# Layer 0 of a graph and experts kernel: the last two second runs of experts go from 160 rows to 128

## The chip, the cores and the metric

The kernel runs on one core of one Trainium2 chip. The metric is the device time of one execution, in microseconds (us). Five engines work side by side, each with its own queue of instructions: TensorE (PE, whose weight loads are listed apart as PEld), VectorE (DVE), ScalarE (ACT), GpSimd (POOL) and SyncE (SP, which here only issues transfers). They meet through semaphores. Transfers between the chip's memory and its on-chip buffers run on 16 DMA engines, fed by queues of SP, ACT and POOL.

## The reference

Two layers, each a graph step and a mixture of experts, on `x` of 3327 tokens with 256 features. All arithmetic is float32. Layer 0, in which the change lies:

```python
x = x + gnn(layernorm(x), adj)                 # a@h / deg @ W.T + b
h = layernorm(x)
probs = softmax(h @ gate_w + gate_b)           # 16 experts
top_probs, top_idx = top_k(probs, 2)           # each token goes to 2 experts
hidden = silu(h @ w1[e]) * (h @ w2[e])         # 256 -> 512
x = x + sum over its 2 experts of prob * (hidden @ w3[e])   # 512 -> 256
```

The reference computes all experts for all tokens and selects; the kernel computes only the two that a token chose. So 2 x 3327 = 6654 pairs of token and expert are spread over 16 experts, 416 each in the mean, and how many each gets depends on the inputs. They come from fixed random seeds.

Layer 1 has a graph attention step and six experts of another form; the change does not touch it.

## The kernel before

**Tiles.** The 3327 tokens make 26 tiles of 128 (the last has 127). Tiles are handled in chunks of four. The graph step runs in three blocks of chunks; the first two (`GRAPH0[:2]`) are tiles 0 to 15, that is tokens 0 to 2047.

**Routing.** When a chunk's graph output is done, `dispatch` chooses two experts per token and writes each pair into a list in memory (`list0`), which has a region of 3328 places for every expert. After tile 15, `filled` (L399) lifts the counter of every expert that has fewer than 256 pairs to 256, so that pairs of later tokens are placed from place 256 on. Places without a pair hold a neutral entry: weight 0, token 0, and as its target one of 256 spare rows behind the result.

**Slots.** The experts' work is done in slots (`plan`, L969). A slot gathers up to 256 rows by its list (`rows_in0`, POOL, L1040), turns them (L1053), multiplies by w1 and w2 (`hidden0`, L1065), applies silu and the product (L1069, L1073), multiplies by w3 (`out0`, L1088), scales (L1093) and adds the rows to the result `xd` in memory (POOL scatter with addition, L1095). There are 32 usual slots:

- slots 0 to 9: the first 256 places of experts 0 to 9, begun while the graph step's last block is being finished;
- slots 10 to 21: experts 10 to 15, which are ranked by their counts (`rank_table`, L409); for each rank one slot of 256 rows and one for its rest;
- slots 22 to 31: the rests of experts 0 to 9, ranked likewise.

The rest of an expert is what stands from place 256 on. How many rows a rest slot takes is fixed by its rank in `WIDTHS`, L100 and L101: six numbers for slots 11, 13, ... 21, then ten for slots 22 to 31. Each slot is cut into parts of 128 rows (`parts0`, L1032): a width of 160 is one part of 128 and one of 32, each with its own gather, turning, w3 matmuls, scaling and scatter.

**The spill table.** `spill_table` (L431) subtracts the width of its rank (`cap`) from each expert's rest. For whatever is left it counts tiles of 256, rounded up, and lists them. Column 3 of its output tells whether there is any. All five engines load that number (`asked`, L562, at slot 30) and branch on it after slot 31 (`more`, L572; the call is at L1236, the branch instructions are recorded at L575). If it is 0, the body is skipped. If it is 1, the body runs: two spill slots of 256 rows, slots 32 and 33, whatever number of pairs they hold, with all parts of a slot; then a second question, whether there are more than two tiles (column 5), and a further body for those; and then, for the six tiles of `HEAD`, a load from `xd`, a layer norm and the weighting that prepares them for layer 1 (`loaded1`, L1158; `weighted1`, L1164).

In the usual case those six tiles are prepared earlier, beside slots 28 to 31 (`head1`, L1189), with loads made on the condition that nothing spills; the graph step of layer 1 can then begin as soon as slot 31 is done. The remaining tiles (`REST`) are loaded after slot 31's scatter has landed.

**What orders the work.** Each engine takes its instructions in the order in which the program was recorded. On POOL, gathers and scatters share one queue, and each waits there for what it needs. A usual slot's scatter waits for its own scaled rows and for the other half of the slot before (`x_added`, `waits`, L1101 to L1105). Spill slots write to `xd` as a whole, so each of their scatters waits for the landing of the one before. On SP, an instruction that waits holds up all loads behind it.

Of the kernel before, what the change touches and what calls it, by code (L numbers as in the profile page):

```python
# [19 lines left out]
P = 128  # L20
# [5 lines left out]
def kernel(  # L26
# [70 lines left out]
    SA = 2 * P  # L97
    AHEAD_E = 5 * E0 // 8
    SHARED = E0 - AHEAD_E
    WIDTHS = [SA, SA - 32, SA - 64, SA - 64, SA - 96, SA - 96]  # L100
    WIDTHS += [SA, SA - 32, SA - 32, SA - 64, SA - 64, SA - 64, SA - 64, SA - 96, SA - 96, SA - 96]  # L101
    assert len(WIDTHS) == E0 and NP % SA == 0
    USUAL0 = 2 * E0
    LATE0 = USUAL0 - 5
    FEW0 = USUAL0 + 2
    SLOTS0 = USUAL0 + (2 * N + E0 * (SA - 1 - min(WIDTHS))) // SA

# [323 lines left out]
    def spill_table(rank, rest, head):  # L431
# [4 lines left out]
        def small(name, w=E0, dtype=F32):  # L436
            return work.tile([P, w], dtype, name=name, bufs=1)

        cap, t, d, end, hot, at = small("x_cap"), small("x_t"), small("x_d"), small("x_end"), small("x_hot"), small("x_at", 2)
        nc.vector.memset(cap, float(WIDTHS[0]))  # L440
        for i in range(1, E0):
            if WIDTHS[i] != WIDTHS[i - 1]:
                nc.vector.tensor_scalar(t, rank, float(i), float(WIDTHS[i] - WIDTHS[i - 1]), op0=OP.is_ge, op1=OP.mult)
                nc.vector.tensor_tensor(cap, cap, t, op=OP.add)
# [1030 lines left out]
```

## Time and profile before

| what | value |
|---|---|
| time, median of 3 runs | 1006.41 us (1002.47 to 1008.44) |
| time of the profiled execution | 1003.44 us |
| its span, first to last instruction | 1001.4 us |
| mean granted TensorE clock | 0.973 |
| busy: PE, PEld, DVE, ACT, POOL | 927.9, 780.5, 486.5, 280.8, 435.4 us |
| layer 0's slots on PE | about 197 to 573 us |
| PE busy in 328 to 573 us | 239.1 of 245 us |
| first matmul of layer 1's graph step | 573.43 us |

How to read it: times are counted from the start of the span. A row of a group names line, engine, operation, tile written and tile read, shapes and how often, then busy time and mean duration, then the idle time of the engine ahead of them and what ended it. In a timeline the first number is the start, the second the duration of merged rows, and what stands in brackets is idle time ahead of it and its releaser. One matmul of the program on float32 data shows as two records of PE. A transfer issued by POOL has a short record on POOL (its issue); when its data have landed is seen from who waits for it.

### The profile page before, as it was taken

The page shows a single profiled execution, that of the slowest core. Times are in us where ns is not written, and L with a number is a line of the kernel's source. Part 1 is how long each engine was busy: PE and PEld are TensorE (multiplying, and loading weights), DVE is VectorE, ACT ScalarE, POOL GpSimd, SP SyncE. Part 2 cuts the span into 40 slices and gives each one's busy share as a digit, 9 for nine tenths or more (in the row PEclk, how much of TensorE's full clock was granted, in tenths as well). Part 3 has the DMA queues.
Part 4 walks back from the last instruction along what each step waited for, and adds up shares of the span by engine and source line. Part 5 has one row for each costly group of instructions (what it writes and reads, how often), then busy time and mean ns, then how long its engine had stood idle before and what let it go on. Part 6 is the DMA issues. An engine that isn't in the chain of part 4 may idle for free. (4 is left out here: it accounts for less than half of the span.)

```text
span 1001.4 us, 14307 instructions
## 1 busy us (share of the span) xinstructions
PE 927.9 (93%) x4506; PEld 780.5 (78%) x4506; DVE 486.5 (49%) x1788; ACT 280.8 (28%) x634; POOL 435.4 (43%) x407
## 2 busy tenths in 40 slices
PE   6899999999998899999999899999999899799981
PEld 5677878778897689888888677787778688678870
DVE  6575585244623222221212657576674764435663
ACT  3311331034311111111111524244132644234330
POOL 2040062522477444545454321000452777777761
PEclk9999999998999899999999999999999999999996
DMA  9998677856676466666988479888975222442376
GB/s 333 327 304 305 232 203 225 257 171 194 170 177 169 124 183 181 178 169 163 263 261 235 132 231 304 287 288 320 269 190 169 61 64 61 66 95 91 96 256 210
DMA packets 104945, 200.56 MB, mean 200 GB/s; under 512 B 30436, under 2 KB 59558, under 8 KB 104864
## 3 DMA queue, kind: packets, MB, share of 16 engines
q1 hardware_dynamic: 64002, 150.87, 46.1%
q0 software_dynamic: 20528, 30.56, 14.2%
q10 hardware_dynamic: 20334, 18.17, 5.7%
q8 instruction: 36, 0.59, 0.2%
q14 instruction: 45, 0.37, 0.1%
HBM read 170.39 MB, written 35.47 MB: 206 GB/s over the span
## 5 line engine op out<-in xcount | busy, mean ns | idle before, releaser
L831 PE MATMUL acc<-big,y 128*128 128x512 f32 (+2 forms) x1456 | 340.2, 388 | 20.7 <-DVE big L705 13.1
L831 PEld LDWEIGHTS acc<-big,y 128*128 128x128 f32 (+1 forms) x1456 | 262.7, 192 | 78.5 <-issue 14.0
L1065 PE MATMUL acc<-xT,w 128*128 128x256 f32 (+3 forms) x1024 | 215.9, 364 | 0.0
L1065 PEld LDWEIGHTS acc<-xT,w 128*128 128x128 f32 x1024 | 187.2, 201 | 17.3 <-issue 3.5
L384 POOL DMA_INDIRECT list<-where,t_idx x104 | 110.6, 1063 | 148.7 <-DVE t_idx L381 96.5
L705 DVE TENSOR_SCALAR big<-adj 128x1536 fp32r<-128x1536 int32 (+5 forms) x128 | 111.3, 873 | 100.1 <-DMA adj<-in_adj_t 55.1
L1088 PE MATMUL acc<-w,hid 128*128 128x256 f32 (+3 forms) x512 | 118.3, 381 | 0.0
L1073 DVE TENSOR_TENSOR hid<-hid,acc 128x512 f32<-128x512 f32 (+3 forms) x64 | 40.0, 624 | 149.4 <-PE acc L1065 142.3
L1095 POOL DMA_INDIRECT xd<-y,who x44 | 68.8, 1563 | 100.1 <-DVE y L1093 58.5
L1088 PEld LDWEIGHTS acc<-w,hid 128*128 128x128 f32 (+3 forms) x512 | 89.2, 178 | 20.5 <-issue 3.9
L1069 ACT ACTIVATE hid<-acc 128x512 f32<-128x512 f32 (+3 forms) x64 | 35.0, 547 | 207.1 <-PE acc L1065 193.8
L627 POOL DMA_INDIRECT zd<-y,who x58 | 71.5, 1233 | 27.8 <-DVE y L1323 12.2
L1309 ACT ACTIVATE h<-acc,v 128x256 f32<-128x256 f32 x116 | 54.8, 473 | 90.9 <-PE acc L1306 90.4
L601 POOL DMA_INDIRECT xg<-hd,who x58 | 59.5, 1027 | 42.3 <-issue 36.2
L1306 PE MATMUL acc<-h,v 128*128 128x256 f32 x232 | 60.6, 384 | 1.8 <-ACT h L1309 1.8
L1306 PE MATMUL acc<-xT,v 128*128 128x256 f32 x232 | 60.7, 383 | 0.0
L1095 POOL DMA_INDIRECT xd<-y,whos x20 | 32.3, 1616 | 65.0 <-DVE y L1093 46.9
L289 POOL TENSOR_TENSOR ln_var<-ln_var,half 128x2 f32<-128x2 f32 (+2 forms) x19 | 16.0, 844 | 100.7 <-DVE ln_var L287 77.6
L1318 PE MATMUL acc<-v,h 128*128 128x256 f32 x232 | 59.7, 403 | 0.1
L1321 DVE TENSOR_TENSOR y<-acc,v 128x512 f32<-128x512 f32 x29 | 20.0, 690 | 69.4 <-PE acc L1318 69.4
L1306 PEld LDWEIGHTS acc<-h,v 128*128 128x128 f32 x232 | 44.3, 199 | 9.1 <-ACT h L1309 2.6
L1040 POOL DMA_INDIRECT xg<-hd,who x44 | 43.0, 976 | 17.8 <-issue 11.0
(300 smaller groups left out, 987.9 us busy)
## 6 DMA issues: line engine op xcount, KB each, us to landing
adj<-in_adj_t SPq DMA_DIRECT2D x58, 768.0 KB, 5.9
w<-in_ffn_w SPq DMA_DIRECT2D x78, 512.0 KB, 6.5
adj<-in_adj_t SPq DMA_DIRECT2D x25, 639.5 KB, 5.8
adj<-in_adj_t SPq DMA_DIRECT2D x25, 512.0 KB, 4.9
adj<-in_adj_t SPq DMA_DIRECT2D x12, 767.0 KB, 5.7
hd<-ln_h ACTq DMA_DIRECT2D x12, 512.0 KB
w_all<-w1d SPq DMA_DIRECT2D x6, 898.0 KB, 7.8
w1d<-in_ffn_w ACTq DMA_DIRECT2D x18, 256.0 KB, 4.9
```

The costliest lines, as they stand in the source:

```text
L384: ins = nc.gpsimd.indirect_dma_start(out=rows_of[2 * (t0 + j) + i], out_offset=bass.IndirectOffsetOnAxis(ap=idx[:, i, j : j + 1], axis=0), ...
L601: last["pool"] = nc.gpsimd.indirect_dma_start(out=xg[:, h, :], out_offset=None, in_=of, in_offset=bass.IndirectOffsetOnAxis(ap=who[:, h, 1 ...
L627: last["pool"] = nc.gpsimd.indirect_dma_start(out=zviews[n * s + h], out_offset=bass.IndirectOffsetOnAxis(ap=who[:, h, 0:1], axis=0), in_= ...
L705: last["mask"] = nc.vector.tensor_scalar(mask[:kr, :, :cols], a[:kr, :, :cols], value, None, op0=op)
L831: last["graph"] = nc.tensor.matmul(acc[c][k][:, :w], y[:kr, j, part, k * P : (k + 1) * P], mask[:kr, jj, i0 : i0 + w], start=(j == 0 and p ...
L1040: last["pool"] = nc.gpsimd.indirect_dma_start(out=xg[:m, h, :], out_offset=None, in_=hd_of[0][: NE0 * P, :] if s < AHEAD_E else hd[:, :], ...
L1065: last["slot"] = nc.tensor.matmul(q[:, c, :n], w[:, k, h0 : h0 + 2 * P - 1 : 2], xT[:, k, :n], start=(k == 0), stop=(k == KD - 1))
L1088: nc.tensor.matmul(ps[:m, h, :], hid[c // 2][:, c % 2, h * P : h * P + m], w3[:, c // 2, c % 2, :], start=(c == 0), stop=(c == NC0 - 1))
L1095: ins = last["pool"] = nc.gpsimd.indirect_dma_start(out=xd_of[2 + h] if s < USUAL0 else xd, out_offset=bass.IndirectOffsetOnAxis(ap=who[s] ...
L1306: ins = nc.tensor.matmul(ps[:, c, :], w[:, k, c : H1 : NC1], src[:, k, :], start=(k == 0), stop=(k == 1))
L1309: last["act"] = nc.scalar.activation(dst[:, c, :], ps[:, c, :], AF.Relu, bias=early["w"][s % 3][:, BB + 2 * i + c : BB + 2 * i + c + 1])
L1318: nc.tensor.matmul(ps[:, h, :], h2[:, c, h * P : (h + 1) * P], w[:, c, :], start=(c == 0), stop=(c == NC1 - 1))
```

## The change

Two numbers in `WIDTHS` change: the rest of the emptiest of experts 10 to 15 (slot 21) and that of the emptiest of experts 0 to 9 (slot 31) are given 128 rows instead of 160.

```diff
-    WIDTHS = [SA, SA - 32, SA - 64, SA - 64, SA - 96, SA - 96]
-    WIDTHS += [SA, SA - 32, SA - 32, SA - 64, SA - 64, SA - 64, SA - 64, SA - 96, SA - 96, SA - 96]
+    WIDTHS = [SA, SA - 32, SA - 64, SA - 64, SA - 96, P]
+    WIDTHS += [SA, SA - 32, SA - 32, SA - 64, SA - 64, SA - 64, SA - 64, SA - 96, SA - 96, P]
```

Three things follow in the program:

- slots 21 and 31 have one part instead of two, and their w1 and w2 matmuls are 128 columns wide instead of 160;
- `spill_table` has two more steps in its sequence of widths (four more small DVE instructions), and treats as spilled what the two rests have above 128;
- `SLOTS0`, which uses the smallest width, goes from 63 to 65, which lengthens the innermost body by two slots.

These are the functions that use the numbers:

```python
def parts0(s):
    n = plan[s][-1]
    return [(h, min(P, n - h * P)) for h in range(-(-n // P))]

# in spill_table; rest = count - 256
nc.vector.tensor_tensor(t, rest, cap, op=OP.subtract)
nc.vector.tensor_scalar(nt, t, float(SA - 1), 0.0, op0=OP.add, op1=OP.max)
nc.vector.tensor_scalar(nt, nt, SA.bit_length() - 1, None, op0=OP.arith_shift_right)
...
nc.vector.tensor_scalar(out[:, 3:4], end[:, E0 - 1 :], 0.0, m, op0=OP.is_gt, op1=OP.max)
nc.vector.tensor_scalar(out[:, 5:6], end[:, E0 - 1 :], float(FEW0 - USUAL0), None, op0=OP.is_gt)

# after the usual slots
with more(*early["more"]):
    list(slots0(USUAL0, FEW0))
    with more(*asked(early["spill"], 0, 5, "many")):
        list(slots0(FEW0, SLOTS0))
    for g in HEAD:
        loaded1(g)
        weighted1(pools1[0], g, norm(g))
```

## The prediction

> **What bounds the kernel now.** First the page's groups by line.
>
> ```profile
> span 1001.4 us, 14307 instructions
> PE 927.9 (93%) x4506; PEld 780.5 (78%) x4506; DVE 486.5 (49%) x1788; ACT 280.8 (28%) x634; POOL 435.4 (43%) x407
> ...
> L1095 POOL DMA_INDIRECT xd<-y,who x44 | 68.8, 1563 | 100.1 <-DVE y L1093 58.5
> ...
> L1095 POOL DMA_INDIRECT xd<-y,whos x20 | 32.3, 1616 | 65.0 <-DVE y L1093 46.9
> ...
> L1040 POOL DMA_INDIRECT xg<-hd,who x44 | 43.0, 976 | 17.8 <-issue 11.0
> ```
>
> PE sets the pace. The scatters number 44 + 20 = 64, two for each of 32 slots: nothing spills today, the body behind the branch is skipped. Next, PE's timeline at slots 19 to 22, which tells what a narrow slot costs.
>
> ```profile
> 463.61 2.35 PE L1065 MATMUL acc<-xT,w 128*128 128x160 f32 x16
> 465.79 3.62 PE L1088 MATMUL acc<-w,hid 128*128 128x256 f32 x16
> 469.24 2.34 PE L1065 MATMUL acc<-xT,w 128*128 128x160 f32 x16
> 471.42 0.60 PE L1053 MATMUL mm<-ident,xg 128*128 128x128 f32 x4
> 471.86 3.65 PE L1065 MATMUL acc<-xT,w 128*128 128x256 f32 x16
> 475.34 3.73 PE L1088 MATMUL acc<-w,hid 128*128 128x256 f32 x16
> ```
>
> Rows follow without gaps: slot 21 is bound by PE. A half of its hidden layer takes 2.17 us from start to start (463.61 to 465.79), its w3 product (475.34) 3.7 us. Third, the passage from layer 0 to layer 1.
>
> ```profile
> 572.95 0.48 DVE L1093 TENSOR_SCALAR y<-acc,who 128x256 f32<-128x256 f32 x1 [0.22 <-PE acc L1088]
> 573.43 0.50 PE L831 MATMUL acc<-big,y 128*128 128x512 f32 x1 [0.52 <-ACTq L575]
> 574.94 1.56 POOL L1095 DMA_INDIRECT xd<-y,who  x1 [3.75 <-DVE y L1093]
> 576.14 34.10 PE L831 MATMUL acc<-big,y 128*128 128x512 f32 x141 [2.20 <-DVEq L575]
> 576.80 1.34 POOL L1095 DMA_INDIRECT xd<-y,who  x1 [0.30 <-issue]
> 581.46 1.42 SPq L1162 DMA_DIRECT2D xs<-xd  x3
> 586.79 0.74 DVE L284 BATCH_NORM_STATS2 ln_st<-xs 128x6 f32<-128x256 f32 x2
> ```
>
> Slot 31 ends on PE at 572.9, layer 1's graph step begins 0.5 us later and runs on, because its first six tiles were prepared before; the last scatter lands beside it. Fourth, that stretch in windows: after the busy times come the granted clock (third number from the end), the DMA engines' share and their GB/s.
>
> ```profile
> 576.00:578.00 2.00, 1.86 (x4) 1.49 (x5) 0.00 (x0) 0.00 (x0) 1.70 (x2) 0.50 0.52 67
> 578.00:580.00 2.00, 2.00 (x7) 1.58 (x6) 0.00 (x0) 0.00 (x0) 0.14 (x1) 0.66 0.26 28
> ```
>
> After 3 us of near idleness PE got half its clock until about 579.3. Fifth, the branch, L575; the two times behind the durations are the starts of its first and second passing, and the first is ours.
>
> ```profile
> L575 SPq COMPARE_BRANCH x2: 73/73/73, 559.3 to 976.7; - x2
> L575 POOLq COMPARE_BRANCH x2: 63/70/77, 575.3 to 982.0; - x2
> L575 POOLq INC_SWDGE_SEM x2: 1153/1177/1201, 580.1 to 985.5; - x2
> ```
>
> SP reaches the branch at 559, long before POOL.
>
> **Does anything spill?** No view tells counts, so I worked them out from the reference's inputs, in double precision, with the lifting to 256 after token 2047. The rests of experts 10 to 15, ranked, are 203, 175, 160, 160, 134, 132; those of experts 0 to 9 are 255, 200, 184, 177, 172, 165, 160, 155, 149, 140. All fit today's widths, which agrees with the 64 scatters. Of the new ones two don't: 132 is 4 above 128, 140 is 12. That is one tile each, two together: column 3 becomes 1, column 5 (more than two) stays 0. The body runs with two full slots for 16 pairs. For both to fit, 16 pairs would have to choose otherwise; the smallest distance between a token's second and third choice is 4.5e-5 in the logits, so one or two may.
>
> **What the Trainium skill says.** "TensorE: Matmul & The Clock Gate", in "Part 1: The HAM clock gate", has PE fall to 1.2 GHz after an idle window of about 3.4 us and return after as much work; the 0.50 above agrees. The same page's "LDWEIGHTS (loading the stationary operand)" gives columns / 1.2 ns, 107 ns for 128, which bounds narrow matmuls from below. "DMA: Bandwidth & Descriptors", "Anatomy of one DMA — SWDGE (gpsimd) path", gives about 2.0 us fixed for a transfer from POOL, most of it until the write is confirmed; the trace has more: scatters land 3.7 us after their start at the least, 6.5 in the median.
>
> **The change part by part**, on the clock of the profiled execution.
>
> 1. Narrow slots. A half goes from 2.17 to about 1.74 us (256, 192 and 160 columns took 3.57, 2.71 and 2.17; 16 weight loads of 107 ns are 1.71), twice 0.43; eight of 16 w3 records go, 1.8; two turnings 0.2. So 2.9 us a slot, 5.8 for both; bounds 4 and 6.5. Two gathers and two scatters of POOL go too, beside PE. Slot 31 then ends at 572.9 - 5.8 = 567.1.
> 2. Four DVE instructions more in the spill table, near 0.2 us each, at slot 12: DVE is busy a quarter of that stage, and the first reader comes at slot 28. Nothing. The condition now skips the early loads of six tiles; their norms still run, on old rows, unused.
> 3. Slot 31's scatter. It waits for slot 30's second. Slot 30's rows are ready near 564.4, its scatters go at 564.7 and 566.6, landing 3.7 later: 570.3, and 1.6 to issue: 571.9. Only then does POOL, in order, reach the body's gathers.
> 4. Four gathers, 1.0 + 0.3 each: the last starts at 576.1. Landing takes 2.8 / 4.5 / 7.9 (least, median, most); the DMA engines are quiet here, I take 4.0: 580.1. Both slots are turned before the first multiplication, so PE waits for the last one.
> 5. PE: turning 0.5; four halves at 3.57 and two w3 products at 3.65 are 21.6, half a microsecond for the last silu; the half clock costs 1.5 more. It runs from 580.1 to 604.2. The 3 MB of weights hide: SP takes the branch by 559, their buffers come free between 558 and 567, each takes 6.5 us. Uncovered they would cost some 10 us.
> 6. Scatters, each waiting for the one before. Slot 32's product ends at 596.4, its rows are scaled at 597.4. Four times start to landing at 4.2 (3.7 seen at the least, 5.1 between 569.83 and 574.94 at the most): 614.2. Slot 33's rows, ready at 605.2, wait for slot 32's scatters, so this chain sets the end.
> 7. Semaphores are put right on POOL behind the inner branch (1.2), then the six tiles are loaded, 5.4 as in the trace (581.46 to 586.79): 620.9.
> 8. Norm and weighting of six tiles, whose steps stand interleaved: DVE statistics 2.6 (four tiles took 1.74), a chain of 15 small steps of 0.2 with the other group's between, 3.3; ACT 6 x 0.52; a function table 1.28; exp, cast and the first tile's two halves 1.7. Together 12.0: layer 1 begins at 632.9.
>
> Before, it began in effect at 575.9 (576.14 less the one matmul done earlier). Both restarts find a half clock. The loss is 57.0, the 5.8 saved included. After that, layer 1 has the same work; its further tiles load behind the six and have 17 us of matmuls to get ready. So 1003.4 + 57 = 1060.4 for a profiled execution; the median of the runs shown is 3.0 above the profiled one: **1063 us**.
>
> Bounds of the unknowns: landing of gathers 2.8 to 5.5 (-1 to +1.5); four scatters 3.5 to 5.1 (-3 to +4); tile load 4 to 6.5 (-1.5 to +1); norm chain 9.5 to 14 (-2.5 to +2); POOL's and PE's start in the body, for which the trace has no taken branch, 0 to 3 (a skip cost DVE 1.5 after its last row); rows that all gather token 0, 0 to 3; the narrow slots -1 to +2. All low gives 1054, all high 1080.
>
> **Rivals.**
> - Nothing spills, the other sign: both smallest rests are at most 128. Then only step 1 remains, 1006.4 - 5.8 = 1000.6. The skipped branch of before can't tell; the counts speak against it. It decides if both 132 and 140 are wrong.
> - The body overlaps better than I read: POOL gathers without waiting for slot 31's scatter, scatters overlap. Then 567.1 is followed by 6 for gathers, PE's 23.6, 6 for the last scaling and scatter, load and norm, 5.4 + 12: 620, a loss of 44, 1050. POOL's order and the wait of each scatter speak against it.
> - The body costs more: three branches whose code each engine has to fetch, and landings as in the loaded stage (6.5 instead of 4.2, four times +9; +8 for fetches): 1080 or more. For it: the loaded median; against it: DMA engines at 0.03 to 0.52 near 575.
>
> **How the numbers follow.** My case 0.71 (1053 to 1077), better overlap 0.08, dearer 0.18, no spill 0.03. The range, 1050 to 1081, leaves out the third, half of the dearer and most of the better overlapped one. A measurement of this kernel tells some 0.5%, 5 us, from no change: slower 0.96, same 0.01 (a spill never comes that cheap; narrow slots that save half might), faster 0.03.
>
> **What would show it.** 66 scatters: 62 of usual slots and 4 of the body; 66 gathers; w3 weight loads of 32 columns down from 40 records to 24; two L1015 loads of w1, w2 and w3 each more (84 of w instead of 78); PE nearly idle from 567 to 580 and from 604 to 633, half clock after both; the six tiles' loads (L1162) a second time, near 615, and DVE L1178 again; the same graph step after it. Wrong if the scatters are 62, or if layer 1 starts before 620 or after 645.

## The result, and the profile after

The changed kernel takes 1071.15 us in the median of 6 runs (1061.05 to 1074.22); the kernel before, run beside it, 1007.13 (6 runs, 1002.47 to 1017.63). The ratio is 1.064, 95% interval 1.059 to 1.069, so the change makes the kernel slower. The profiled execution took 1070.83 us, at a mean clock of 0.951 (0.973 before).

The page's groups that answer to those of before:

```profile
span 1069.0 us, 14663 instructions
...
PE 950.9 (89%) x4590; PEld 801.4 (75%) x4590; DVE 499.7 (47%) x1858; ACT 292.7 (27%) x658; POOL 440.8 (41%) x411
...
L1095 POOL DMA_INDIRECT xd<-y,who x46 | 72.1, 1568 | 135.7 <-DVE y L1093 64.4
...
L1095 POOL DMA_INDIRECT xd<-y,whos x20 | 32.2, 1612 | 62.6 <-DVE y L1093 44.6
L1040 POOL DMA_INDIRECT xg<-hd,who x46 | 45.2, 982 | 18.0 <-issue 12.5
```

There are 46 + 20 = 66 scatters: two halves fewer in the usual slots, four more in the body. So the body ran, on two spill slots. PE has 23 us more work, and the span is 68 us longer. PE's timeline at slot 21, the first narrow one:

```profile
471.37 3.62 PE L1088 MATMUL acc<-w,hid 128*128 128x256 f32 x16
474.82 2.04 PE L1065 MATMUL acc<-xT,w 128*128 128x128 f32 x16
476.70 0.61 PE L1053 MATMUL mm<-ident,xg 128*128 128x128 f32 x4
...
480.63 1.89 PE L1088 MATMUL acc<-w,hid 128*128 128x256 f32 x8
482.36 3.62 PE L1065 MATMUL acc<-xT,w 128*128 128x256 f32 x16
487.39 0.74 PE L1053 MATMUL mm<-ident,xg 128*128 128x128 f32 x4 [1.42 <-DMA xg<-hd,who]
```

A half of the hidden layer takes 1.88 us from start to start (474.82 to 476.70; 2.17 before), and the w3 product has 8 records instead of 16 (1.7 us to the next row, 3.7 before). But 5 us later PE waits 1.42 us for gathered rows, as it did not in the kernel before. The passage to layer 1, from the timeline of all engines (the first two rows are SP's, of the body: the lists of the spill slots and their weights):

```profile
563.76 1.72 SPq L983 DMA_DIRECT2D who<-list  x2
566.28 8.30 SPq L1015 DMA_DIRECT2D w<-in_ffn_w  x6
...
572.12 2.05 PE L1088 MATMUL acc<-w,hid 128*128 128x256 f32 x8
...
575.12 1.36 POOL L1095 DMA_INDIRECT xd<-y,who  x1 [0.30 <-issue]
...
582.30 1.56 POOL L1095 DMA_INDIRECT xd<-y,who  x1 [5.82 <-SPq L575]
584.17 1.00 POOL L1040 DMA_INDIRECT xg<-hd,who  x1 [0.30 <-issue]
...
588.02 0.95 POOL L1040 DMA_INDIRECT xg<-hd,who  x1 [0.30 <-issue]
...
592.82 0.70 PE L1053 MATMUL mm<-ident,xg 128*128 128x128 f32 x2 [0.56 <-DMA xg<-hd,who]
593.32 12.97 PE L1065 MATMUL acc<-xT,w 128*128 128x256 f32 x48
...
610.55 1.64 POOL L1095 DMA_INDIRECT xd<-y,who  x1 [21.58 <-DVE y L1093]
613.03 3.87 PE L1088 MATMUL acc<-w,hid 128*128 128x256 f32 x16
615.61 1.58 POOL L1095 DMA_INDIRECT xd<-y,who  x1 [3.43 <-DMA xd<-y,who]
...
620.04 1.55 POOL L1095 DMA_INDIRECT xd<-y,who  x1 [2.85 <-DMA xd<-y,who]
624.56 1.54 POOL L1095 DMA_INDIRECT xd<-y,who  x1 [2.96 <-DMA xd<-y,who]
629.85 2.83 SPq L1162 DMA_DIRECT2D xs<-xd  x5
634.04 0.75 DVE L284 BATCH_NORM_STATS2 ln_st<-xs 128x6 f32<-128x256 f32 x2 [16.23 <-DMA xs<-xd]
...
644.35 5.90 PE L831 MATMUL acc<-big,y 128*128 128x512 f32 x14 [27.44 <-ACT y L1177]
```

Read it from the top: slot 31 ends on PE at 572.12 + 2.05 = 574.17. Slot 31's scatter starts 8.1 us later, the four gathers behind it; the last gathered rows reach PE at 592.82, PE ends at 616.90, the four scatters go one after the other, then the six tiles are loaded and normalised, and the graph step begins at 644.35. From the end of slot 31 to the graph step in earnest it is 70.2 us; before, 572.91 to 576.14, 3.2. That is where the loss lies. (The row of 582.30 names SP's queue as what ended POOL's idle time. By the order of the program, the scatter waits for the landing of slot 30's second one, of 575.12; in e9 below, the same kernel, its row reads `[5.59 <-DMA xd<-y,who]`.) Two rows of PE's waits hold most of it:

```profile
PE acc L831 <- ACT y L1177: 27.4, 1, 27.4
PE mm L1053 <- DMA xg<-hd,who: 21.6, 8, 13.9
```

The first names ACT, the last link of a chain of scatters, loads and normalisation; the second holds 13.9 us ahead of the body. The windows, with granted clock, DMA share and GB/s at the end, first one of the kernel before, then three of the changed one:

```profile
570.00:580.00 10.00, 7.28 (x24) 4.67 (x24) 2.68 (x9) 3.27 (x8) 4.08 (x3) 0.83 0.32 39
```

```profile
570.00:580.00 10.00, 4.17 (x25) 3.24 (x24) 5.25 (x20) 5.61 (x11) 2.92 (x2) 0.89 0.92 250
580.00:590.00 10.00, 1.09 (x4) 0.63 (x4) 0.00 (x0) 0.00 (x0) 5.45 (x5) 0.50 0.42 63
590.00:600.00 10.00, 8.19 (x26) 6.30 (x25) 0.51 (x1) 3.05 (x4) 0.00 (x0) 0.59 0.18 18
```

And the branch's group, with times of its first and last passing:

```profile
L575 SPq COMPARE_BRANCH  x4: 43/61/73, 562.8 to 1044.4; - x4
...
L575 POOLq COMPARE_BRANCH  x4: 43/66/68, 582.1 to 1049.7; - x4
...
L575 POOLq INC_SWDGE_SEM  x2: 1248/1306/1365, 628.4 to 1053.0; - x2
```

The DMA engines were not quiet when slot 30's scatter had to land: 0.92 busy in 570 to 580, against 0.32 in that window before. SP had taken the branch at 562.8 and was loading the body's weights. POOL came to the branch at 582.1, 19 us later.

Outside these places the executions differ without the change's doing: layer 0's first slot began 8.9 us later in the second profile (218.4 against 209.5), its slots up to 18 took 2.4 us less, and slots 22 to 28 took 0.4 us more. Two experiments on one chip speak against the change as the reason for the later beginning: e2, with the widths of before, begins at 224.4, e4, with the new ones, at 224.1. After the passage both run alike: 68.2 us apart at the start of the graph step, 67.6 at the end.

### The profile page after: what moved, and what is told of

Same layout as the page of the kernel before. It is cut to its first block, busy times and chain, and to the rows that moved or that the text cites. A ratio compares the mean times of both kernels' runs of the same rounds, so it can differ in the third digit from the quotient of the medians.

```text
span 1069.0 us, 14663 instructions
## 1 busy us (share of the span) xinstructions
PE 950.9 (89%) x4590; PEld 801.4 (75%) x4590; DVE 499.7 (47%) x1858; ACT 292.7 (27%) x658; POOL 440.8 (41%) x411
## 4 chain that ended last, share of the span: by engine, by line
PE 43%; DMA 17%; DVE 8%; issue 7%; POOL 6%; ACT 1%; POOLq 0%; SPq 0%; DVEq 0%; ACTq 0%
PE acc L1065 13%; PE acc L831 9%; DMA xg<-hd,who 8%; PE acc L1088 7%; PE acc L1306 4%; PE mm L772 3%; PE acc L1318 3%; DMA zd<-y,who 2%; POOL list L384 2%; DMA list<-where,t_idx 2%; DVE big L705 2%; DMA adj<-in_adj_t 2%; PE mm L1259 1%; PE mm L1053 1%; DMA xd<-y,who 1%
## 5 line engine op out<-in xcount | busy, mean ns | idle before, releaser
L1065 PE MATMUL acc<-xT,w 128*128 128x256 f32 (+4 forms) x1088 | 229.9, 365 | 0.0
L1065 PEld LDWEIGHTS acc<-xT,w 128*128 128x128 f32 x1088 | 199.8, 202 | 18.5 <-issue 3.1
L1095 POOL DMA_INDIRECT xd<-y,who x46 | 72.1, 1568 | 135.7 <-DVE y L1093 64.4
L1073 DVE TENSOR_TENSOR hid<-hid,acc 128x512 f32<-128x512 f32 (+4 forms) x68 | 42.4, 624 | 175.7 <-PE acc L1065 168.5
L1088 PE MATMUL acc<-w,hid 128*128 128x256 f32 (+3 forms) x528 | 122.0, 381 | 0.0
L1088 PEld LDWEIGHTS acc<-w,hid 128*128 128x128 f32 (+3 forms) x528 | 93.5, 181 | 19.7 <-issue 3.3
L1069 ACT ACTIVATE hid<-acc 128x512 f32<-128x512 f32 (+4 forms) x68 | 37.2, 547 | 216.8 <-PE acc L1065 191.6
L627 POOL DMA_INDIRECT zd<-y,who x58 | 71.5, 1232 | 27.4 <-DVE y L1323 11.5
```

What stands on the lines that cost most here:

```text
L627: last["pool"] = nc.gpsimd.indirect_dma_start(out=zviews[n * s + h], out_offset=bass.IndirectOffsetOnAxis(ap=who[:, h, 0:1], axis=0), in_= ...
L1065: last["slot"] = nc.tensor.matmul(q[:, c, :n], w[:, k, h0 : h0 + 2 * P - 1 : 2], xT[:, k, :n], start=(k == 0), stop=(k == KD - 1))
L1088: nc.tensor.matmul(ps[:m, h, :], hid[c // 2][:, c % 2, h * P : h * P + m], w3[:, c // 2, c % 2, :], start=(c == 0), stop=(c == NC0 - 1))
L1095: ins = last["pool"] = nc.gpsimd.indirect_dma_start(out=xd_of[2 + h] if s < USUAL0 else xd, out_offset=bass.IndirectOffsetOnAxis(ap=who[s] ...
```

## The experiments

Two theories stood against each other. Mine: the loss is the body behind the branch, a chain with its own first and last waits, and it is paid in full once anything spills. Rivals: the loss goes by what spills (pairs or tiles); the narrow slots themselves cost something; or one single wait of the chain is most of it.

The runs were made in four groups on three chips: e1 to e4, e5 to e8 (both on one chip), e9 to e11, and e12. In the first two groups the kernel before took 1063 to 1065 us, in the last two 1000.6 and 1004.2, so that runs are compared by ratio within a group, or by the passage in the trace: the time from the end of slot 31's last matmul to the graph step. A passage is read from one profile per run; the changed kernel's two profiles give 70.2 and 68.4 us, so differences under 2 us tell nothing.

**e1, the narrow slots without a spill.** The widths of the change, but the spill table keeps the caps of before; the 16 pairs are left out.

```diff
+    CAPS = [max(w, SA - 96) for w in WIDTHS]
...
-        nc.vector.memset(cap, float(WIDTHS[0]))
+        nc.vector.memset(cap, float(CAPS[0]))
...
```

The lines left out put `CAPS` for `WIDTHS` in the loop that follows, too.

> Slots 21 and 31 are narrow, but the spill table keeps the widths of before, so that the 16 pairs above 128 are left out of the result and the body is skipped. Theory (the loss is the body, the narrow slots gain): slot 31 ends about 7.6 us earlier in relation to the first slot than before, time 0.992 to 0.996 of before, 62 scatters. Rival (the narrow slots or the longer program cost something themselves, such as the 8.9 us by which the changed kernel's profile was late at its first slot): time 1.000 or more, first w1 matmul again near 218 us.

Measured: 1.0002 (0.995 to 1.0054). The expected gain (0.992 to 0.996) is not seen. There are 62 scatters, so the halves are gone. Slot 31 ends 2.6 us earlier in relation to the first slot than in the kernel before, where 7.6 was expected: slot 21 won only 0.4 us (PE waits 2.5 us for the gathered rows behind it). And at the passage (lines are one higher in this kernel):

```profile
584.92 2.09 PE L1089 MATMUL acc<-w,hid 128*128 128x256 f32 x8
...
588.53 0.90 ACT L1178 ACTIVATE y<-ln_h,w 128x255 fp32r<-128x255 f32 x2
...
589.53 0.50 PE L832 MATMUL acc<-big,y 128*128 128x512 f32 x1 [2.52 <-ACTq L576]
...
592.50 0.80 PE L832 MATMUL acc<-big,y 128*128 128x512 f32 x1 [2.46 <-DVEq L576]
```

PE is done at 587.01 but ACT weights the last of the six tiles until 589.43, and then takes the branch; the passage is 5.5 us instead of 3.2. Slot 31 won 3.0 us and gave 2.3 back. So about 1 us of 5.8 is left at the graph step, less than these runs can tell.

**e2, the body with nothing in it.** The widths of before; the condition is made true for zero.

```diff
-        nc.vector.tensor_scalar(out[:, 3:4], end[:, E0 - 1 :], 0.0, m, op0=OP.is_gt, op1=OP.max)
+        nc.vector.tensor_scalar(out[:, 3:4], end[:, E0 - 1 :], 0.0, m, op0=OP.is_ge, op1=OP.max)
```

> The widths of before, nothing spills, but column 3 of the spill table is always 1: the body runs on two slots of neutral rows. Theory: the body costs what it does in the changed kernel whatever pairs it holds, 66 to 70 us between the end of slot 31 and layer 1's graph step, time 1.062 to 1.072 of before. Rival (the price lies in the pairs that spill, or in the real experts' weights): below 1.05.

Measured: 1.069 (1.060 to 1.078), passage 67.2 us, from the end of slot 31's last product to the graph step:

```profile
583.89 3.79 PE L1088 MATMUL acc<-w,hid 128*128 128x256 f32 x16
...
654.89 35.36 PE L831 MATMUL acc<-big,y 128*128 128x512 f32 x145 [26.98 <-ACT y L1177]
```

No pair spills, and the loss is the same.

**e3, one narrow slot.** Slot 21 alone; four pairs, one tile.

```diff
-    WIDTHS = [SA, SA - 32, SA - 64, SA - 64, SA - 96, SA - 96]
+    WIDTHS = [SA, SA - 32, SA - 64, SA - 64, SA - 96, P]
```

> Only slot 21 is narrow, slot 31 has 160 rows again: 4 pairs spill, one tile. Theory: both slots of the body run all the same, so the loss stays and grows by what slot 31 no longer saves, time 1.064 to 1.072 of before. Rival (the loss goes by spilled tiles): about half, 1.03 to 1.035.

Measured: 1.072 (1.064 to 1.080), passage 68.0 us. The loss does not go by tiles or pairs: half of it was the rival's forecast.

**e4, the body without its weights.** The changed kernel, the spill slots multiply by whatever weights lie there.

```diff
-        last["who"] = nc.sync.dma_start(w0[plan[s][0] % 2][i], w)
+        if s < USUAL0:
+            last["who"] = nc.sync.dma_start(w0[plan[s][0] % 2][i], w)
```

> The changed kernel, but the body loads no weights (3 MB); its slots multiply by what slots 30 and 31 left, so the 16 pairs get wrong values. Theory of the missed term (slot 31's scatter stood 5.8 us behind slot 30's landing because the body's own weights filled the DMA engines): that scatter starts 4 to 6 us earlier in relation to the end of slot 31, and the passage gets as much shorter, time 4 to 7 us below the changed kernel's. Rival (the wait is the branch, or POOL's turn, not the DMA engines): no earlier, time within 2 us of the changed kernel's.

Measured: 1.066 (1.056 to 1.075), passage 65.2 us. POOL's timeline (lines one higher), slot 30's second scatter and slot 31's:

```profile
584.15 1.36 POOL L1096 DMA_INDIRECT xd<-y,who  x1 [0.30 <-DVE y L1094]
587.71 1.56 POOL L1096 DMA_INDIRECT xd<-y,who  x1 [2.20 <-DMA xd<-y,who]
```

From start to start 3.56 us; 7.18 in the changed kernel, 6.67 in e2, 6.69 in e3. So the weights nearly double the time in which that scatter lands. Slot 31's scatter starts 4.5 us after the end of slot 31, in the changed kernel 8.1 us: 3.7 us earlier, a little less than the 4 to 6 expected. In all the passage is 2 to 5 us shorter. (The changed kernel was not run in this group, so the times can't be compared.) The spread has a reason that the traces show: after the idle stretch PE's granted clock is 0.50 until some point in the body's work, 5.5 us after the arrival of the last rows in the changed kernel (592.82 to 598.27), 3.2 in e9, 3.8 in e4. As an estimate, PE loses half of that time. Without it the passages are 67.5, 66.8 and 63.3 us, and e4's is shorter by 3.5 to 4.1 us: nearly all of it is the one scatter.

**e5, the six tiles kept.** The early load is made whatever spills, and the body doesn't repeat it.

```diff
-        nc.vector.tensor_scalar(out[:, 4:5], out[:, 3:4], -1.0, 1.0, op0=OP.mult, op1=OP.add)
+        nc.vector.tensor_scalar(out[:, 4:5], m, -1.0, 1.0, op0=OP.mult, op1=OP.add)
...
-        for g in HEAD:
-            loaded1(g)
-            weighted1(pools1[0], g, norm(g))
```

> The changed kernel, but the early load and the normalisation of the six tiles that the graph step of layer 1 needs first are kept whatever the rests are, and the body no longer repeats them (on this input no pair of these six tiles lies in a spill slot, so the result is the same; on another it could be wrong). Theory: the scatters of the spill slots stay, but nothing of the first part of the graph step waits for them. The 27 us by which PE waited for ACT behind the body's own matmuls goes; the matmuls of the graph step begin some 3 us after the body's last matmul, and PE waits later, for the ten other tiles, some 6 us at most. So 20 to 27 us below the changed kernel, about 1.040 to 1.048 of the kernel before, with 36 to 45 us between the last matmul of slot 31 and the graph step instead of 70. Rival, that the landing of the four scatters sets the graph step's end in any case, because the ten other tiles wait for the same scatters: then under 8 us are won and the ratio stays above 1.058.

**e6, the scatters by halves.**

```diff
-                    out=xd_of[2 + h] if s < USUAL0 else xd,
+                    out=xd_of[2 + h] if s < FEW0 else xd,
...
-            if s < USUAL0:
+            if s < FEW0:
```

> The changed kernel, but the four scatters of the two spill slots go out through the two disjoint halves of the rows, as those of the usual slots do, and wait for the other half of the slot before alone. Theory of a serial chain: in the changed kernel each of the four waits for the landing of the one before (17.9 us from the first one's start to the last one's landing); in pairs, one landing and one issue fall out of the chain: 4 to 6 us less, so 64 to 66 us in the passage instead of 70 and a ratio 0.004 to 0.006 lower than the changed kernel's. Rival, that the hardware's queue does the four one after the other whatever they wait for: no change in the 17.9 us.

**e7, one spill slot.** With the widths of e3.

```diff
-    FEW0 = USUAL0 + 2
+    FEW0 = USUAL0 + 1
```

> One narrow slot (slot 21 alone) and a spill table of one slot of 256 pairs instead of two; the four spilt pairs of the ten experts fit in it. Theory: the body's matmuls halve (24.1 to about 12), two of four scatters fall out of the chain (8 to 9 us), the weights are half, so that the body's first gathers come no later: the passage from slot 31's last matmul to the graph step falls from 68 us (the same widths with two spill slots) to 46 to 50, ratio 1.050 to 1.056. Rival, that the passage is set by the one-off costs (landing before the gathers, loads and normalisation of the six tiles): not under 58 us.

Measured, e5 to e7: the runs of before in this group lay between 1033 and 1071 us, so their times (1096.3, 1122.9 and 1102.2 against 1065.5, quotients 1.029, 1.054 and 1.034) have no interval. All three miss the ratios expected, on the low side, by about 12, 5 and 17 us that the passages don't explain. A part lies behind layer 1's graph step, which no edit touches: in the profiles the stretch from its last matmul to the end takes 242 to 248 us in e5 to e7, but 254 to 257 in e1 to e4 and e8 on the same chip. The passages can be read: 41.1 us in e5, with 6.45 us of waiting in the middle of the graph step; 64.0 in e6; 49.6 in e7. These are as expected, e5's later wait half a microsecond above. The two rows of e5:

```profile
580.80 2.12 PE L1088 MATMUL acc<-w,hid 128*128 128x256 f32 x8
...
623.98 16.70 PE L831 MATMUL acc<-big,y 128*128 128x512 f32 x72 [0.56 <-PEq L575]
```

In e6 the scatters go in pairs:

```profile
620.17 1.64 POOL L1095 DMA_INDIRECT xd<-y,who  x1 [21.53 <-DVE y L1093]
622.11 1.58 POOL L1095 DMA_INDIRECT xd<-y,who  x1 [0.31 <-issue]
627.33 1.55 POOL L1095 DMA_INDIRECT xd<-y,who  x1 [3.63 <-DVE y L1093]
629.19 1.54 POOL L1095 DMA_INDIRECT xd<-y,who  x1 [0.30 <-issue]
```

From the first scatter's start to the tiles' loads it is 14.3 us (620.17 to 634.48) against 19.3 in the changed kernel. So the serial landing was the kernel's order, not the queue's; the second pair now waits for DVE, that is for PE's own end.

**e9, the changed kernel again, as yardstick on another chip; e10, e5 and e6 together; e11, those and one spill slot.**

> The changed kernel itself, on the chip of the experiments, as their yardstick. If the loss is the passage and nothing else, its ratio lies at 1.064 to 1.070, its passage from the last matmul of slot 31 to the graph step of layer 1 at 68 to 71 us (70.2 in its first profile), and slot 31's scatter starts 6.5 to 7.5 us after slot 30's second one. Rival, that the experiments' low ratios (1.029 without the renormalisation, 1.034 with one spill slot) come from the call and not from the edits: then it is below 1.055 here.

> The two edits together: the six tiles' early load and normalisation kept, and the scatters of the spill slots through disjoint halves. In the kernel with the first edit alone PE waited 6.45 us in the middle of the graph step for the tiles that are loaded after the last scatter's landing. Theory, that the chain of four scatters in a row sets this wait: with two pairs the landing comes 4 to 5 us earlier and the wait falls to 1 to 3 us; the passage itself stays at 40 to 42 us, since PE's own end sets it. Ratio 0.003 to 0.006 below the kernel with the first edit alone. Rival, that the loads and the normalisation of these tiles set the wait: it stays above 5 us.

> Those two edits and one spill slot in place of two (slot 21 alone narrow, four pairs spill): the cheapest way of spilling that these edits give. The body's matmuls are 12 to 13 us, the gathers before them start some 5 us after the end of slot 31 (the body has half the weights to load), so the passage is 22 to 26 us, with no wait later in the graph step. Against 3.2 us in the kernel before this still loses some 20 us: ratio 1.018 to 1.026. Rival, that a later wait, for the tiles behind the last scatter, comes back: then 1.03 or more.

| | ratio (95%) | passage, us | wait in the graph step, us |
|---|---|---|---|
| e9, changed kernel | 1.068 (1.061 to 1.075) | 68.4 | - |
| e10, six tiles kept, scatters by halves | 1.044 (1.036 to 1.052) | 43.6 | 3.0 |
| e11, one spill slot besides | 1.022 (1.013 to 1.031) | 24.5 | 2.9 |

e9 is what was expected: slot 31's scatter starts 6.95 us after slot 30's second. The low quotients of the second group lie with that group: e10, with nearly e5's passage and wait (46.6 and 47.5 us together), has 1.044 here, e5 1.029 there. Here passages and ratios agree: from e9 to e11 passage and wait fall by 41.0 us, 4.1% of 1000.6, the ratio by 4.6 points. Three rows of PE's waits, one of e5, one of e10, one of e11:

```profile
PE acc L831 <- DVE ln_st L284: 6.4, 1, 6.4
```

```profile
PE acc L831 <- DVE ln_mv L285: 3.0, 1, 3.0
```

```profile
PE acc L831 <- ACT y L1177: 2.9, 1, 2.9
```

With the tiles kept, the chain of scatters is still waited for, by the ten other tiles. The pairs of e10 halve this wait. That one slot would end it was wrong: it stays at 2.9, in e11. e10's passage is 1.6 us over its range and 2.5 us longer than e5's: its gathers start 10.5 us after slot 31 where e5's start 9.3, and the half clock lasts 5.6 us into the body's work where it lasts 2.8 in e5 (some 1.4 us, an estimate by half of the difference). In e11, with half the weights, they start 4.7 us after it.

**e8 and e12, narrow to the rows without a spill.** Widths that hold every rest of this input, six notches of 32 rows fewer than before:

```diff
-    WIDTHS = [SA, SA - 32, SA - 64, SA - 64, SA - 96, SA - 96]
-    WIDTHS += [SA, SA - 32, SA - 32, SA - 64, SA - 64, SA - 64, SA - 64, SA - 96, SA - 96, SA - 96]
+    WIDTHS = [SA - 32, SA - 64, SA - 96, SA - 96, SA - 96, SA - 96]
+    WIDTHS += [SA, SA - 32, SA - 64, SA - 64, SA - 64, SA - 64, SA - 96, SA - 96, SA - 96, SA - 96]
```

> The kernel before with six notches of 32 rows fewer, at widths that still hold every rest of this input (224, 192, 160, 160, 160, 160 and 256, 224, 192, 192, 192, 192, 160, 160, 160, 160): nothing spills. By PE's arithmetic, 6 times 0.87 us of w1 and x1 matmuls: 5 us fewer, ratio 0.995. Rival, after the narrow slots without a spill gained nothing (1.0002): slots late in the row are waited for by DVE, ACT and the rows' gathers, so that the time saved comes back as waits of PE: ratio 0.998 to 1.002.

> The widths of six notches of 32 rows fewer, without a spill, once more: the first call gave no interval, since its chip's runs lay too far apart. In its trace the passage was as short as in the kernel before (3.4 us against 3.2), and one slot's rows came late (PE idle 1.8 us, then at a lower clock). Theory, that PE's arithmetic counts where no wait takes over: 3 to 5 us fewer, ratio 0.995 to 0.997. Rival, that the slots' other engines and transfers take it back: 0.998 to 1.002.

Measured: e8 1063.0 against 1065.5, without an interval; e12 0.998 (0.9955 to 1.0008, 22 runs against 27). The rival's value; a gain of 0.4% is not excluded, none is shown. From slot 12 to the end of slot 31 e12 takes as long as the kernel before (188.6 and 188.4 us): it is 2.4 us ahead at slot 24 and gives that back in two places, where PE waits for rows. One of them, in the timeline:

```profile
540.84 8.66 SPq L1015 DMA_DIRECT2D w<-in_ffn_w  x6
...
544.46 0.90 POOL L1040 DMA_INDIRECT xg<-hd,who  x1 [0.30 <-issue]
...
549.30 0.50 PE L1053 MATMUL mm<-ident,xg 128*128 128x128 f32 x2 [0.74 <-DMA xg<-hd,who]
...
550.33 0.42 PE L1053 MATMUL mm<-ident,xg 32*128 32x32 f32 x2 [0.53 <-DMA xg<-hd,who]
```

The gather of 544.46 is usable at 550.33, 5.9 us later, beside six loads of weights. PE waits 1.3 us in these two rows, and from 551.75 to 555.16 its granted clock is 0.50. PE had been made faster than its rows arrive.

## Why the prediction was right

1063 us were predicted, 1071 measured: slower, by the mechanism named. As a ratio 1063 is 1.056 of before, below the measured interval, so the loss was put too low. By its steps, each measured in the profile after:

| step | predicted, us | measured, us |
|---|---|---|
| 1, both narrow slots | -5.8 | -5.5 |
| 3, end of slot 31 to the end of its scatter's issue | 4.8 | 9.7 |
| 4, gathers, to the last landing | 8.2 | 9.0 |
| 5, PE in the body | 24.1 | 24.1 |
| 6, from PE's end to the last scatter's landing | 10.0 | 11.5 |
| 7, semaphores, load of six tiles | 6.7 | 5.6 |
| 8, norm and weighting | 12.0 | 10.3 |
| passage, 3 to 8 | 65.8 | 70.2 |

- **Whether anything spills** decided the sign, and the counts were right: two spill slots ran, as 66 scatters and 84 loads of weights (78 before) show. e2 and e3 show that the number of pairs then doesn't matter.
- **Step 1** had the right size by luck of two errors: between the w3 products of slots 18 and 22 1.5 us were won, not 2.9, since PE then waits 1.42 us for rows. (The 2.9 had put a narrow half at 1.74 us; it takes 1.88.) Their second gather starts at 480.89 and they are there at 487.39, 6.5 us later; in the kernel before PE came for them 7.2 us after it (475.32 to 482.57) and found them. The DMA engines are full there in both (share 1.05 before, 1.06 after), with weights and the adjacency. All ten profiles with a narrow slot 21 show this wait, 1.0 to 2.5 us, and none of before, e2, e8 and e12 does. From slot 28 on 4.1 us were won, where two waits of the kernel before (0.56 and 0.29 us) are gone besides. e1 shows what it is worth alone: about 1 us. The rival "nothing spills", put at 1000.6 us, would by its ratio have come out near 1006.
- **Step 2**, nothing for the DVE instructions, was not tested by itself; no wait near slot 12 shows it.
- **Step 3** was mis-sized, and is the largest miss. The landing of slot 30's scatter was put at 3.7 us, the least of the trace, and "the DMA engines are quiet here" (step 4) was read from the kernel before, in which SP had nothing to load at that time. In the body SP, 19 us ahead of POOL, loads 3 MB. Slot 30's second scatter landed after 7.2 us, not 3.7 (without the loads 3.6 in e4 and 4.1 in e1). The other 1.4 us are that this scatter started later in relation to the shorter slot. The Trainium skill, "DMA: Bandwidth & Descriptors", in "SWDGE vs HWDGE vs iDMA", says that POOL's and SP's transfers go through different queues of the same DMA engines, which take turns; e4 agrees with it, 3.1 to 3.6 us for this scatter.
- **Step 5** said that the weights "hide". For PE's matmuls they do. That the sum was met to the tenth is luck: the half clock lasted longer into the body (0.50 until 598.27) and cost 2.0 us instead of 1.5, the w3 products and the wait for the last silu 0.5 less than put. The price of the weights was in step 3, with another transfer.
- **Step 6**: 3.8 to 5.1 us a scatter, 4.5 in the mean, in place of 4.2. That they are serial because each waits for the whole of `xd` is shown by e6.
- **Steps 7 and 8** were 1.1 and 1.7 us too dear. That this chain is on the path is shown by e5: without it the passage falls to 41 us.
- The bound of 0 to 3 us for entering the body on POOL was not needed: its first gather starts 0.3 us behind the scatter, like one issue after another. So of the rival by which the body costs more, entering it cost nothing that shows on the path, and landings were late for one scatter (7.2 us), not for the four of the body (4.5 us each, where 6.5 was put).

The sum of the changes, 67.0 - 5.5 = 61.5 us, agrees with the medians (64 us, interval 60 to 69); 57.0 were predicted. The passage was put 4.4 us too short, and that it was not more is luck in part: steps 3, 4 and 6 were 7.2 us too cheap, steps 7 and 8 2.8 us too dear. The 68.2 us between the two profiles at the start of the graph step hold 6.8 us of the differences named above. They also brought the start of layer 1, at 644.35, to within 0.65 us of the mark of 645 that was to show the prediction wrong. What stays open: why on one chip the stretch behind the graph step is so much longer and varies so much, and with it the second group's quotients.

## What to carry to other kernels

A width that is a capacity has a price on each side: what a narrower slot saves on PE, at best some 3 us here and often less because the rows come no faster, and what one row too many costs, 64 to 67 us of passage in one piece (the changed kernel, e2, e3 and e9, less the 3.2 us of before) whatever the number of rows. So count the rows for the inputs at hand before judging such a notch, and price the rare branch as a chain of its own, ends included. Where a branch is taken early by the engine that issues loads, those loads run beside the tail of the work before it: ask which transfer there is waited for. If the rare case must be cheaper, this chain gave back most by keeping prepared what doesn't depend on it (about 20 us; e5's edit does so for this input alone and could be wrong on another), then by fewer slots (19 us in the passage), then by scatters of a slot's two halves, whose rows differ, in pairs (4 to 6 us); all together 1.022 instead of 1.068.

## What the runs showed of the hardware that was not expected

- A scatter with addition of 32 rows let the one that waits for it start after 3.6 us in e4 and 4.1 us in e1, without weight loads beside it (the DMA engines moved 48 GB/s meanwhile), and after 6.7 to 7.7 us beside weight loads (198 to 253 GB/s; changed kernel, e2, e3, e5, e6, e9, e10); gathers took 5.9 and 6.5 us to be usable beside such loads (e12, changed kernel).
- Two scatters with addition to different rows overlap: start to start 1.9 us (e6), against 4.4 to 5.1 in the changed kernel, where each waits for the landing before.
- The kernel before takes 1000 to 1007 us beside the result, e9 to e11 and e12, and 1063 to 1065 on the chip of e1 to e8. About half of the difference lies behind layer 1's graph step: that stretch takes 224 us in the kernel before and 254.6 and 256.6 in e1 and e8, PE is idle for 39 and 40 us of it instead of 18, up to 7.5 us at a time and in part without anything in the profile that it waits for, and its granted clock is 0.83 to 0.92 in most windows of 40 us instead of 0.92 to 1.00. Which causes which is not shown.
